# A graph layer's sort by destination group: whole quads sorted by 16 permute matmuls, or halves sorted by 8 and regrouped by DMA

## The chip, the cores and the metric

The kernel runs on one core of one Trainium2 chip. Times are microseconds (us) of the device for one execution; the median of the runs shown is compared. Engines: PE (TensorE), DVE (VectorE), ACT (ScalarE), POOL (GpSimd) and SP (SyncE, which issues most DMAs). SBUF is the on-chip memory with 128 partitions, PSUM holds the matmuls' sums.

## The reference

One message-passing layer on 6250 nodes of 128 features and 200,000 edges (`src`, `dst`, the latter sorted), with 20 edge features each:

```python
h = relu(layernorm(x))
x = h @ W_in
W_ij = (ssp(f_ij @ W_f1 + b_f1) @ W_f2 + b_f2) * f_ij_cutoff   # ssp(z) = softplus(z) - log 2
x_ij = x[idx_j] * W_ij                                         # a row of 128 for each edge
out = segment_sum(x_ij, idx_i, 6250)
result = x_in + (ssp(out @ W_o1 + b_o1) @ W_o2 + b_o2)
```

`idx_i` is `src` (in no order), `idx_j` is `dst` (sorted). So the gather reads neighbouring rows, and the sum over `src` scatters to anywhere.

## The kernel before, in words

**Quads.** The edges are taken in chunks of 128 and quads of 4 chunks (512 edges), 391 quads; two quads share one load of 1024 edges (`load_sc`, L338). One iteration of the main loop (L1325) handles one quad at each stage of a pipeline: in iteration i, quad i gets its one-hot matrix and filter exponentials, quad i-1 its messages, older quads the steps behind. The order of work on each engine is written out by hand: every step is put at an iteration and at a named point in it (`at`, `put`, the table `AT` at L34). The points run in the order L, D0, D1, PE0, PEZ, AE, A0, A1, AX, DM, DR, PE1, PE2, A2, D2, S (L1325 to L1379). Each engine, SP with its DMAs included, goes through its own part of this order without overtaking.

**Gather.** For each quad SP loads windows `wn` of 21 consecutive nodes (63 rows of a table in device memory, three bfloat16 parts to a node), one for each 256 edges (`WSEG`): 4 DMAs in a `load_sc`. The place comes from a register that SP loads from `base_i` and multiplies by 3 (L351 to L356). A one-hot matmul (`s2_pe_x`, L545) picks the rows, and DVE multiplies them with the filter (`s2_m`, L570): that is the messages.

**Scatter, three ways.** The first 12 "plain" quads that are not sorted merge edges of equal `src` within a chunk by an equality matrix (`s1_eq`, L401) and scatter-add 128 rows for each chunk. The other 188 plain quads are "listed": DVE compares the sources with `sb`, the row of sources broadcast to all partitions (`sb_load`, L386; `l_eq`, L419), edges with a repeated source go to a list, and the messages are scattered as they are. POOL issues each scatter as an indirect DMA with accumulation (`scatter`, L636), 4 for a quad, into one of up to four accumulators `acc` in device memory in turn (`acc_of`, L623: three in turn up to the 170th scatter, then four, and three again for the last 64).

**Sorting.** Every second quad from 8 to 388 (191 quads, `sorted_quads`, L1584) is sorted instead. The 6250 nodes make 16 groups of 392 (`GN`). `rank_group` to `rank_slot` (L645 to L713) give each of the 512 edges a slot: 32 (`CAP`) for each group, 512 in all, and 64 (`OVC`) more for what doesn't fit. `perm_oh` (L715) writes the one-hot matrix `pm`, 4 chunks x 576 columns. The messages are split in three bfloat16 parts (`part_rem`, L730) and carry their node number (`part_ext`). `permute` (L741) multiplies, for each of 4 blocks s of 128 slots, all 4 chunks: 16 matmuls of 387 columns. `perm_out` (L748) copies each block from PSUM by ACT to `ms` (one tile for each s). `over_pe` (L752) and the steps behind it take the overflow of two sorted quads as one more scatter of 128 rows. After 8 sorted quads (a round, `RND`), `unit_oh` and `unit_pe` (L820, L830) turn the sorted rows into sums: for each s 96 matmuls on 32 partitions each, a group to each 32, which DVE adds to `accT` in SBUF (`unit_evac`, L844). `unit_slots` (L1600) chooses the iterations of these units, the first of them `ULAG` = 5 after the round's last quad or the next free one.

**Sources.** `src16` in device memory holds the sources as int16, in the edges' order: `load_idx`, `src_cast` (L869, L890) make its first half at the start, `half_load`, `half_piece` (L1041, L1048) the second half in two pieces of the first iterations, together with the places `reld` of the destinations in their windows (`rel`, L938).

**End.** The accumulators are read back and summed, the output layers follow (L1478 on). If an edge found no slot or lay outside its window, a flag makes a slow loop over all 1563 chunks run (L1400 on).

Of the kernel before, what the change touches and what calls it, by code (L numbers as in the profile page):

```python
# [7 lines left out]
F32 = mybir.dt.float32  # L8
# [17 lines left out]
OVC = 64  # L26
SLOTS = GRP * CAP + OVC
# [5 lines left out]
ULAG = 5  # L33
AT = {  # L34
# [40 lines left out]
def tile_gnn(ctx: ExitStack, tc: tile.TileContext, x, fB, cT, srcT, srcr, srci, dstr, win_, wf1, wf2, bias, bo1c, wo1,  # L75
# [30 lines left out]
    mbufs = [max(len(qs) + sum(q > qs[-1] and (q + 3 if q + 4 in units else q + 4 + s // 2) <= us[s] for q in mpq) for qs, us in zip(rounds, uslots))  # L106
             for s in range(4)]
    splain = [q for q in range(NQ) if q not in mpi]
    plain = {q: n for n, q in enumerate(splain)}
    NS = len(splain)  # L110
    LB, LE = listed(NS) if spread else (0, 0)
# [68 lines left out]
    for i in range(2):  # L180
        ext_ = cp.tile([P, 4 * RKQ, 3], BF16, name=f"ext{i}")
        exts.append(ext_)
# [154 lines left out]

    def load_sc(s):  # L338
# [9 lines left out]
        for j in range(nh):  # L348
            nc.sync.dma_start(rb[j * HB:(j + 1) * HB], reld[s:s + 1, j * SEG:(j + 1) * SEG].to_broadcast([HB, SEG]))
        wn = ld.tile([P, 2, P], BF16, tag="wn", name="wn")  # L350
        _, regs = nc.values_load_multi_w_load_instructions(  # L351
            base_i[pp:pp + 1, hh, 0:2 * nh], engines=[SP], min_val=0, max_val=top,
            skip_runtime_bounds_check_because="clamped on the chip to [0, top]")
        for k in range(2 * nh):
            j, c = divmod(k, 2)
            nc.sync.dma_start(wn[j * HB:j * HB + NR, c, :], tab[bass.ds(regs[k] * 3, NR), :])  # L356
# [29 lines left out]
    def sb_load(k):  # L386
        qs = splain[2 * k:2 * k + 2]
        t_ = ld.tile([P, 2 * SEG], I16, tag="sb", name="sb", bufs=4)
        for j, q in enumerate(qs):
            if j and q == qs[0] + 1 and q % 2:  # L390
                continue
            n = 2 if j == 0 and len(qs) > 1 and qs[1] == q + 1 and q % 2 == 0 else 1
            o = q % 2 * SEG
            nc.sync.dma_start(t_[:, j * SEG:(j + n) * SEG],
                              src16[q // 2:q // 2 + 1, o:o + n * SEG].to_broadcast([P, n * SEG]))
        sbs[k] = t_
# [4 lines left out]
    def s1_eq(q):  # L401
# [3 lines left out]
        eq = wk.tile([P, 4, P], F32, tag="eq", name="eq", bufs=2)  # L405
# [139 lines left out]
    def s2_pe_x(q):  # L545
# [7 lines left out]
        for c in range(4):  # L553
            nc.tensor.matmul(xg[:, c, :], st[q]["oh"][a:a + NR, c * P:(c + 1) * P], wn[a:a + NR, c // 2, :],  # L554
# [114 lines left out]
    def before_me(ps_t, src, w, own=False):  # L669
        n = src.shape[1]  # L670
        nc.tensor.matmul(ps_t, trib if own else tri, src, start=True, stop=False)
        o = ps_t.rearrange("p (j c) -> p j c", c=4 * w)
# [1072 lines left out]
```

## Time and profile before

| | |
|---|---|
| median of 3 runs | 1914.89 us (1914.53 to 1915.02) |
| the profiled execution | 1913.11 us, its span 1911.3 us |
| instructions | 58065 |
| DMA packets | 351575, 267.55 MB |
| HBM | read 154.65 MB, written 109.00 MB |
| mean granted TensorE clock | 0.979 |

A profile is of one execution. "Busy" is the time in which an engine has an instruction under way. A group's row gives line, engine, operation, written tile <- read tiles, shape, count, then busy us, the mean of one in ns, and the idle time ahead of them with what ended it. Matmuls overlap, so the busy time over the count is what one costs, and the mean is how long one takes from end to end. In a list of waits each row says who waited, for what, us in total, how often, and the longest.

### The profile page before, as it was taken

To read this page: it belongs to the slowest core of one execution; us is meant where nothing else is said; L and a number is where in the kernel's file an instruction comes from. 1 tells how busy PE (TensorE), PEld (TensorE's weight loads), DVE (VectorE), ACT (ScalarE), POOL (GpSimd) and SP (SyncE) were. 2 spreads that over 40 slices of the span, in tenths; PEclk is the share of its full clock that TensorE was granted. 3 is DMA by queue.
4 is the path that set the end of the run, shared out by engine and by line. 5 is a ranking of instruction groups with operands and counts; after the bars stand their busy time and mean duration, and the time that the engine had idled before them with its cause. 6 is when DMAs were issued, how large, how long until landed. Compare 5 with 4: busy or idle time off the path is not lost. (4 is left out here: it accounts for less than half of the span.)

```text
span 1911.3 us, 58065 instructions
## 1 busy us (share of the span) xinstructions
PE 1809.2 (95%) x20601; PEld 1228.2 (64%) x20601; DVE 1655.9 (87%) x4692; ACT 1474.9 (77%) x4045; POOL 1509.0 (79%) x961
## 2 busy tenths in 40 slices
PE   4679999999999999999999999999999999999986
PEld 3556666666666666666666666666666666666654
DVE  5678998899999989999999889889889888888767
ACT  4569788878887878878887787787787787787725
POOL 4578777788888888887777888888888888878755
PEclk8789999999999999999999999999999999999998
DMA  8788777767776777776776667677676667666648
GB/s 287 201 208 167 142 162 135 131 125 131 139 135 123 131 126 130 129 152 116 125 135 126 124 126 129 118 129 129 116 130 129 116 130 127 117 117 133 106 99 269
DMA packets 351575, 267.55 MB, mean 140 GB/s; under 512 B 96655, under 2 KB 315194, under 8 KB 351282
## 3 DMA queue, kind: packets, MB, share of 16 engines
q1 hardware_dynamic: 218516, 197.56, 35.9%
q0 software_dynamic: 132208, 66.05, 34.6%
q8 instruction: 162, 2.65, 0.6%
q14 instruction: 131, 1.07, 0.2%
q10 hardware_dynamic: 558, 0.20, 0.0%
HBM read 154.65 MB, written 109.00 MB: 138 GB/s over the span
## 5 line engine op out<-in xcount | busy, mean ns | idle before, releaser
L639 POOL DMA_INDIRECT acc<-s,lji x751 | 1201.5, 1600 | 267.9 <-issue 174.4
L744 PE MATMUL pq<-pt,pm 128*128 128x387 bf16 x3056 | 583.2, 337 | 1.2 <-ACT s L597 0.6
L567 ACT ACTIVATE xc<-xg,cb 128x128 f32<-128x128 f32 x1564 | 448.1, 376 | 171.5 <-PE xg L554 151.9
L750 ACT CAST mst<-pq 128x387 bf16<-128x387 f32 x764 | 364.0, 487 | 91.7 <-PE pq L744 68.1
L562 PEld LDWEIGHTS W<-w,a 128*128 128x128 f32 x3128 | 421.7, 196 | 17.9 <-issue 7.3
L744 PEld LDWEIGHTS <-pm 128*128 128x128 bf16 x3056 | 294.4, 98 | 197.5 <-issue 4.9
L840 PE MATMUL un<-so,mst 32*128 32x392 bf16 x9168 | 411.3, 325 | 10.0 <-DVE rank L686 2.8
L562 PE MATMUL W<-w,a 128*128 128x128 f32 x3128 | 420.1, 278 | 0.0
L840 PEld LDWEIGHTS <-mst 32*128 32x128 bf16 x9168 | 249.8, 93 | 146.7 <-issue 19.0
L373 ACT ACTIVATE a<-a,con 128x512 f32<-128x512 f32 x391 | 282.5, 723 | 11.6
L733 DVE TENSOR_TENSOR pt<-pt 128x512 f32<-128x512 f32 x382 | 261.0, 683 | 0.0
L719 DVE TENSOR_SCALAR pm<-iotp,pos 128x576 bf16<-128x576 f16 x764 | 255.6, 396 | 0.0
L368 ACT ACTIVATE a<-z 128x512 f32<-128x512 f32 x391 | 236.6, 605 | 5.9 <-PE z L363 5.9
L851 DVE TENSOR_TENSOR accT<-un,accT 128x392 f32<-128x392 f32 x368 | 182.4, 558 | 63.1 <-PE un L840 34.8
L639 POOL DMA_INDIRECT acc<-os,oji x108 | 180.9, 1675 | 51.3 <-issue 12.9
L825 DVE TENSOR_SCALAR so<-iot,mst 128x392 bf16<-128x392 f16 x764 | 215.3, 333 | 2.2 <-PE un L840 1.9
L577 DVE TENSOR_TENSOR pt<-W,xc 128x512 f32<-128x512 f32 x191 | 131.6, 689 | 57.0 <-ACT xc L567 23.9
L363 PE MATMUL z<-ft,ws 123*128 123x512 bf16 x391 | 153.8, 394 | 19.9 <-POOL b2rep L979 8.4
L554 PE MATMUL xg<-wn,oh 63*128 63x128 bf16 x1564 | 156.6, 221 | 13.5 <-DVE oh L380 12.1
L577 DVE TENSOR_TENSOR s<-W,xc 128x512 f32<-128x512 f32 x188 | 128.7, 685 | 45.5 <-ACT xc L567 34.8
L551 PE MATMUL W<-b2rep,onesb 64*128 64x512 bf16 x391 | 152.9, 391 | 0.0
L639 POOL DMA_INDIRECT acc<-s,ji x48 | 81.0, 1688 | 42.1 <-DMA acc<-s,ji 20.5
(215 smaller groups left out, 1796.0 us busy)
## 6 DMA issues: line engine op xcount, KB each, us to landing
rb<-reld SPq DMA_DIRECT2D x391, 64.0 KB
sb<-src SPq DMA_DIRECT2D x192, 128.0 KB
fsd<-f SPq DMA_DIRECT2D x49, 480.0 KB
ft<-fsd SPq DMA_DIRECT2D x195, 120.0 KB
fb<-in_fB_dram SPq DMA_DIRECT2D x49, 320.0 KB
ft<-fsd SPq DMA_DIRECT2D x195, 80.0 KB
wn<-tab SPq DMA_DIRECT2D x782, 15.8 KB
acc<-s,lji POOLq DMA_INDIRECT x751
```

The lines of the kernel that those rows point to most:

```text
L368: nc.scalar.activation(a, st[q]["z"], AF.Exp)
L373: nc.scalar.activation(a, a, AF.Ln, bias=half, scale=0.5)
L562: nc.tensor.matmul(W[:, c, :], st[q]["a"][:, c * P:(c + 1) * P], w2, start=False, stop=(c == 3))
L567: nc.scalar.mul(xc[:, c, :], st[q]["xg"][:, c, :], late["c", q // CQ][:, 4 * (q % CQ) + c:4 * (q % CQ) + c + 1])
L577: nc.vector.tensor_tensor(m[:, :, :P], st[q]["W"], st[q]["xc"], op=ALU.mult)
L639: nc.gpsimd.indirect_dma_start(out=accs[k][:rows, :], out_offset=bass.IndirectOffsetOnAxis(ap=ji, axis=0), in_=s, in_offset=None, compute_ ...
L719: nc.vector.tensor_scalar(pm[:, c], iotp, rk[r]["pos"][:, 4 * j + c:4 * j + c + 1], None, op0=ALU.is_equal)
L733: nc.vector.tensor_tensor(pt[:, :, k * P:(k + 1) * P], a, high(a), op=ALU.subtract)
L744: nc.tensor.matmul(t[:, :PW], mp[q]["pm"][:, c, s * P:(s + 1) * P], high(mp[q]["pt"][:, c:c + 1, :PW])[:, 0], start=(c == 0), stop=(c == 3))
L750: nc.scalar.copy(mp[q]["ms", s][:, :PW], mp[q].pop(("q", s))[:, :PW])
L825: nc.vector.tensor_scalar(so, iotw[:, :GN], w[:, 3 * P // 2:3 * P // 2 + 1], None, op0=ALU.is_equal)
L840: nc.tensor.matmul(ts[g][:, :GN], mp[q]["ms", s][v, k * P:(k + 1) * P], mp[q]["oh"][v], start=(q == qs[0] and k == 0), stop=(q == qs[-1] a ...
```

## The change

Sorted quads are sorted in two halves of 256 edges. Each half has 16 slots (`BCAP`) for each of the 16 groups, 256 in all; overflow has 128 slots, shared by the four halves of two sorted quads. `pm` is 4 x 384. `permute` multiplies, for each half h and each of 2 blocks, the 2 chunks of that half: 8 matmuls of 388 columns. ACT copies the two blocks of a half into a staging tile `sg` (one of three buffers that `eq` has). Two DMAs of 64 partitions for each half (`regroup`), issued by SP, move whole rows of 1552 bytes from `sg` to every second partition of two tiles `ms`, so that 32 partitions again hold one group: 16 rows of the first half, 16 of the second. `regroup` stands at point A1 of iteration q+4 (first half) and q+5 (second); where q+4 is a unit's iteration, all permutes stand in q+3 as before and both regroups at point L of q+4. `ULAG` is 7. `ms` has 11 and 15 buffers of 1552 bytes a partition, where the four tiles had 9, 11, 13 and 15 of 776.

The source rows are put into the plain quads' order on the host: 100 rows, cast once at the start by POOL; `sb_load` is one DMA of both quads. The second half's source loads and casts go.

In the first half of the edges (196 quads) a window serves 512 edges: 2 `wn` DMAs in a `load_sc` in place of 4. `base_3` holds the places times 3, so SP multiplies nothing.

The diff, cut to its core:

```diff
-OVC = 64
-SLOTS = GRP * CAP + OVC
+BCAP = 16
+OVC = 128
+SLOTS = GRP * BCAP + OVC
-ULAG = 5
+ULAG = 7
+    "rg0": (4, "A1"), "rg1": (5, "A1"),
-             for s in range(4)]
+    mbufs = [max(len(qs) + sum(q > qs[-1] and q + 5 <= us[2 * j + 1] for q in mpq) for qs, us in zip(rounds, uslots))
+             for j in range(2)]
+    def seg_of(s):
+        return SEG if spread and s < HALF else WSEG
...
-            base_i[pp:pp + 1, hh, 0:2 * nh], engines=[SP], min_val=0, max_val=top,
-        for k in range(2 * nh):
-            j, c = divmod(k, 2)
-            nc.sync.dma_start(wn[j * HB:j * HB + NR, c, :], tab[bass.ds(regs[k] * 3, NR), :])
+            base_3[pp:pp + 1, hh, 0:m * nh], engines=[SP], min_val=0, max_val=3 * top,
+        for k in range(m * nh):
+            j, c = divmod(k, m)
+            nc.sync.dma_start(wn[j * HB:j * HB + NR, c, :], tab[bass.ds(regs[k], NR), :])
...
     def sb_load(k):
-            nc.sync.dma_start(t_[:, j * SEG:(j + n) * SEG],
-                              src16[q // 2:q // 2 + 1, o:o + n * SEG].to_broadcast([P, n * SEG]))
+        nc.sync.dma_start(t_[:, :n], src16[k:k + 1, :n].to_broadcast([P, n]))
...
-    def before_me(ps_t, src, w, own=False):
+    def before_me(ps_t, src, w, m, own=False):
...
-        nc.vector.tensor_scalar(ov, rank, float(BIG + CAP), None, op0=ALU.is_ge)
+        nc.vector.tensor_scalar(ov, rank, float(BIG + BCAP), None, op0=ALU.is_ge)
...
-    def permute(q, s):
-        for c in range(4):
-            nc.tensor.matmul(t[:, :PW], mp[q]["pm"][:, c, s * P:(s + 1) * P], high(mp[q]["pt"][:, c:c + 1, :PW])[:, 0],
-                             start=(c == 0), stop=(c == 3))
+    def permute(q, k):
+        h, s = divmod(k, 2)
+        for c in (2 * h, 2 * h + 1):
+            nc.tensor.matmul(t[:, :MW], mp[q]["pm"][:, c, s * P:(s + 1) * P], high(mp[q]["pt"][:, c:c + 1, :MW])[:, 0],
+                             start=(c == 2 * h), stop=(c == 2 * h + 1))
-    def perm_out(q, s):
-        mp[q]["ms", s] = wk.tile([P, MW], BF16, tag=f"ms{s}", name="mst", bufs=mbufs[s])
-        nc.scalar.copy(mp[q]["ms", s][:, :PW], mp[q].pop(("q", s))[:, :PW])
+    def perm_out(q, k):
+        h, s = divmod(k, 2)
+        if s == 0:
+            mp[q]["sg", h] = wk.tile([P, 2, MW], BF16, tag="eq", name="sg", bufs=3)
+        nc.scalar.copy(mp[q]["sg", h][:, s], mp[q].pop(("q", k))[:, :MW])
+    def regroup(q, h):
+        sg = mp[q].pop(("sg", h))
+        for j in range(2):
+            if h == 0:
+                mp[q]["ms", j] = wk.tile([P, 2, MW], BF16, tag=f"ms{j}", name="mst", bufs=mbufs[j])
+            nc.sync.dma_start(mp[q]["ms", j][h::2].rearrange("p s f -> p (s f)"),
+                              sg[j * HB:(j + 1) * HB].rearrange("p s f -> p (s f)"))
     def over_pe(q):
-        for c in range(4):
-            for h, p in enumerate(qs):
-                nc.tensor.matmul(t[h * OVC:(h + 1) * OVC, :PW], mp[p]["pm"][:, c, GRP * CAP:],
-                                 high(mp[p]["pt"][:, c:c + 1, :PW])[:, 0], start=(c == 0), stop=(c == 3))
+        for p in qs:
+            for c in range(4):
+                nc.tensor.matmul(t[:, :PW], mp[p]["pm"][:, c, GRP * BCAP:], high(mp[p]["pt"][:, c:c + 1, :PW])[:, 0],
+                                 start=(p == qs[0] and c == 0), stop=(p == q and c == 3))
...
-                    nc.tensor.matmul(ts[g][:, :GN], mp[q]["ms", s][v, k * P:(k + 1) * P], mp[q]["oh"][v],
+                    nc.tensor.matmul(ts[g][:, :GN], mp[q]["ms", s // 2][v, s % 2, k * P:(k + 1) * P], mp[q]["oh"][v],
...
+                for h in range(2):
+                    at(q + 4, "L", regroup, q, h)
...
+                for h in range(2):
+                    put(f"rg{h}", q, regroup, q, h)
...
-        "srci": srcp.reshape(-1, 2, P).transpose(0, 2, 1).reshape(-1, SC),
+        "srci": srcp.reshape(-1, 2, P).transpose(0, 2, 1).reshape(-1, SEG)[order].reshape(-1, SC),
```

More of the change, by code (lines that the diff above doesn't have):

```diff
@@ L110, in tile_gnn @@
     NS = len(splain)
+    SR = -(-NS // 2)
     LB, LE = listed(NS) if spread else (0, 0)
@@ L667, in rank_local @@
         rk[r]["ext"] = ext
[L669 removed]
+    def before_me(ps_t, src, w, m, own=False):
         n = src.shape[1]
         nc.tensor.matmul(ps_t, trib if own else tri, src, start=True, stop=False)
[L672 to L675 removed]
+        parts = []
+        a = n // (m * w) * m * w
+        if a:
+            parts.append((0, a, m))
+        if a < n:
+            parts.append((a, n, (n - a) // w))
+        for a, b, c in parts:
+            o = ps_t[:, a:b].rearrange("p (j c) -> p j c", c=c * w)
+            v = src[:, a:b].rearrange("p (j c) -> p j c", c=c * w)
+            for k in range(1, c):
+                nc.tensor.matmul(o[:, :, k * w:], onesb, v[:, :, :(c - k) * w], start=False,
+                                 stop=(b == n and k == c - 1))
     def rank_count(r):
```

95 lines of the change are left out of this document (43 added, 52 removed), and 2 rows, old and new, of the table AT.

## The prediction

> **What bounds the kernel now.** I read the page's busy line first, then busy time by stage, then what POOL waits for in each stage, and the groups by line last.
>
> ```profile
> PE 1809.2 (95%) x20601; PEld 1228.2 (64%) x20601; DVE 1655.9 (87%) x4692; ACT 1474.9 (77%) x4045; POOL 1509.0 (79%) x961
> ```
>
> By this line TensorE is the bound: it is busy for 95% of the span of 1911.3 us, POOL for 79%. By stage it looks otherwise. The columns are stretch and length, then busy us (and instructions) of PE, PEld, DVE, ACT, POOL, the granted clock, the DMA share and GB/s.
>
> ```profile
> 90.00:400.00 310.00, 294.30 (x3221) 199.34 (x3220) 271.07 (x786) 251.25 (x702) 245.92 (x152) 0.98 0.78 157
> 400.00:800.00 400.00, 391.87 (x4562) 265.90 (x4564) 367.25 (x1082) 325.13 (x907) 335.96 (x211) 1.00 0.72 131
> 1200.00:1700.00 500.00, 495.70 (x5840) 332.92 (x5829) 440.47 (x1232) 403.96 (x1106) 416.73 (x256) 1.00 0.69 124
> ```
>
> POOL's waits between 400 and 800 us (waited for: us in total, times, longest):
>
> ```profile
> POOL acc L639 <- issue: 44.8, 147, 0.3
> POOL acc L639 <- DMA acc<-s,lji: 7.6, 25, 0.3
> ```
>
> No wait there is longer than 0.3 us, and 0.3 us stands ahead of every scatter: it belongs to the instruction. So 211 scatters of 335.96 / 211 = 1.59 us and 0.30 us each are 399 of the 400 us. POOL is saturated there. Between 800 and 1700 us it isn't quite:
>
> ```profile
> POOL acc L639 <- DVE s L577: 25.3, 25, 2.3
> POOL acc L639 <- DVE srcf L650: 3.5, 2, 2.4
> POOL acc L639 <- DVE bn L234: 2.3, 2, 2.0
> ```
>
> Less 0.3 us for each of the 29 times, 31.1 - 8.7 = 22.4 us is real waiting for a message that DVE had yet to make. From 1700 to 1840 us:
>
> ```profile
> POOL acc L639 <- DVE s L577: 6.6, 5, 4.1
> POOL acc L639 <- DMA acc<-s,lji: 6.5, 7, 3.0
> POOL acc L639 <- ACT pt L739: 4.3, 2, 3.6
> ```
>
> This is 10.9 - 2.1 = 8.8 us for messages, and 4.4 us for earlier scatters. Two engines are thus level: PE at 98 to 99% of every stage and POOL within 3% of it. Time taken from PE alone can bring back only what POOL waits for PE's results, some 31 us, and not what PE is relieved of.
>
> **The change part by part.** The groups (busy us, mean ns; the z row is of 300 to 1800 us alone):
>
> ```profile
> L639 POOL DMA_INDIRECT acc<-s,lji x751 | 1201.5, 1600 | 267.9 <-issue 174.4 <-DVE s L577 33.4 <-DMA acc<-s,lji 28.0
> L639 POOL DMA_INDIRECT acc<-os,oji x108 | 180.9, 1675 | 51.3 <-issue 12.9 <-DMA acc<-s,lji 9.7 <-ACT oji L814 9.4
> L639 POOL DMA_INDIRECT acc<-s,ji x48 | 81.0, 1688 | 42.1 <-DMA acc<-s,ji 20.5 <-issue 7.6 <-ACT a L368 5.5
> L744 PE MATMUL pq<-pt,pm 128*128 128x387 bf16 x3056 | 583.2, 337 | 1.2 <-ACT s L597 0.6 <-ACT mst L750 0.6
> L757 PE MATMUL po<-pt,pm 128*64 128x387 bf16 x764 | 86.6, 344 | 7.7 <-DVE accT L851 4.0 <-DVE so L825 1.7 <-issue 1.0
> L719 DVE TENSOR_SCALAR pm<-iotp,pos 128x576 bf16<-128x576 f16 x764 | 255.6, 396 | 0.0
> L733 DVE TENSOR_TENSOR pt<-pt 128x512 f32<-128x512 f32 x382 | 261.0, 683 | 0.0
> L825 DVE TENSOR_SCALAR so<-iot,mst 128x392 bf16<-128x392 f16 x764 | 215.3, 333 | 2.2 <-PE un L840 1.9 <-issue 0.3
> L750 ACT CAST mst<-pq 128x387 bf16<-128x387 f32 x764 | 364.0, 487 | 91.7 <-PE pq L744 68.1 <-issue 19.1
> L363 PE MATMUL z<-ft,ws 123*128 123x512 bf16 x329 | 128.1, 389 | 4.0 <-DVE pt L577 4.0
> ```
>
> The z row gives the pace: 1500 us / 329 = 4.56 us for a quad, 9.12 us for a pair (one sorted, one listed).
>
> *TensorE.* A permute multiplies 2 chunks in place of 4: 1528 of 3056 matmuls go, at 583.2 / 3056 = 0.191 us, so -292 us. The overflow matmuls stay 764 but are 128 columns wide; at 64 wide two of them share the array and one costs 86.6 / 764 = 0.113 us. Between 0.113 and 0.191 I take 0.191, the row of that width: +60 us. PE falls to about 1577 us.
>
> *VectorE.* pm has 384 columns for 576. By columns 255.6 us becomes 170, so -85 us; if the fixed part were all of it, 0. I take -75. DVE then has some 1580 us.
>
> *ScalarE.* The 764 copies at L750 keep their size. Nothing.
>
> *POOL.* All 751 + 108 + 48 = 907 scatters remain. They and their 0.3 us are 1463 + 272 = 1735 us, which PE at 1577, DVE at 1580 and ACT at 1475 no longer reach: POOL alone becomes the bound from its first scatters on. The waits for messages go: -22 us (800 to 1700) and -9 us (1700 to 1840). What is late next is POOL's own last scatter, and the chain behind it (list rows read back, summed, scattered, tail), which I leave as it is. Nothing is gained from 400 to 800 us, where nothing waited.
>
> *Sources and windows.* Sorting the source rows on the host makes one DMA of each pair of sb, and one window for each of the first 196 quads takes 196 wn DMAs away. The casts of the second half leave DVE, one tiny multiplication comes. All of this is on SP and DVE, which have room: 0 us, and at most the 1 us that SP's shorter first loads may bring at the start.
>
> *The regroup.* 191 x 4 = 764 DMAs of 64 rows x 1552 bytes, 75.9 MB, are new. They have two costs, on SP and on the DMA engines. Rows of the DMA view, and two pairs of SP's timeline (start, us, what):
>
> ```profile
> q1 hardware_dynamic: 218516, 197.56, 35.9%
> sb<-src SPq DMA_DIRECT2D x192, 128.0 KB
> wn<-tab SPq DMA_DIRECT2D x782, 15.8 KB
> ```
> ```profile
> 1005.46 0.91 SPq L394 DMA_DIRECT2D sb<-src  x2
> 1047.69 1.88 SPq L349 DMA_DIRECT2D rb<-reld  x2
> 1052.51 1.09 SPq L345 DMA_DIRECT2D ft<-fsd  x3
> 1053.69 1.11 SPq L349 DMA_DIRECT2D rb<-reld  x2
> 1055.87 1.76 SPq L356 DMA_DIRECT2D wn<-tab  x4
> ```
>
> No transfer from SBUF to SBUF is in the trace, so both prices are bounded. On SP an issue lies between 0.36 (ft) and 0.56 us (rb, also 64 rows); I take 0.5, nearer to rb. A pair now holds SP for 1.09 + 1.11 + 1.76 us, up to 1.1 us between rb and wn, and some 0.5 us of sb: 5.5 us. With four regroups 7.5 us, under 9.12. In SP's order the first two wait for ACT's copies at A0 of iteration q+4 and the others at q+5, and behind them stand the loads of the next iterations, which are needed three iterations later (13 us): that is their cover. Twice in each 16 iterations a regroup has to wait for the unit matmuls to release its ms buffer; SP then stands until the end of that iteration, when the same cover has some 8 us left. If the cover were gone, PE would stop, but POOL would still have the messages of up to six s buffers to scatter.
>
> On the DMA engines the new share is 48,896 / 218,516 x 35.9% = 8% by packets or 75.9 / 197.56 x 35.9% = 14% by bytes. I take 11%, between the two since 1552 bytes is above q1's mean of 904; the wn that go give back under 1%. The share goes from 0.72 to about 0.82. That matters to POOL, which waits for an earlier scatter into the same accumulator. Between 90 and 400 us, with three accumulators in turn and a share of 0.78:
>
> ```profile
> POOL acc L639 <- DMA acc<-s,lji: 13.8, 17, 2.2
> POOL acc L639 <- DMA acc<-s,ji: 6.3, 7, 2.5
> POOL acc L639 <- DMA acc<-os,oji: 1.7, 2, 0.8
> ```
>
> Less 26 x 0.3 us this is 14.0 us on 152 scatters. With 11% more traffic I take it at 23, +9 us (bounds 0 and +30). From 400 us on four accumulators take turns, and no wait is over 0.3 us even at 0.72: 0 there.
>
> *POOL's own speed.* Three scatters, and DVE at that time:
>
> ```profile
> 1121.08 2.01 POOL L639 DMA_INDIRECT acc<-os,oji  x1 [0.30 <-ACT mst L750]
> 1123.39 1.54 POOL L639 DMA_INDIRECT acc<-s,lji  x1 [0.30 <-DVE ovs L771]
> 1125.24 1.69 POOL L639 DMA_INDIRECT acc<-s,lji  x1 [0.30 <-issue]
> ```
> ```profile
> 1118.15 1.20 DVE L719 TENSOR_SCALAR pm<-iotp,pos 128x576 bf16<-128x576 f16 x4
> 1120.99 0.69 DVE L733 TENSOR_TENSOR pt<-pt 128x512 f32<-128x512 f32 x1
> 1125.14 1.40 DVE L719 TENSOR_SCALAR pm<-iotp,pos 128x576 bf16<-128x576 f16 x4
> ```
>
> A scatter takes 1.54 us undisturbed; 2.01 with an L733 begun just before it, 1.69 beside four pm instructions, which then take 1.40 in place of 1.20. All scatters together lose 1463.4 - 907 x 1.54 = 67 us so. If L733, L719 and L825 share that by their 732 busy us, pm has 23 us of it, and a third of it goes with its columns: 8 us. The sharing is a guess, so I take half: -4 us.
>
> The Trainium skill, in "SBUF — State Buffer", section "Who interferes with whom", says that DVE instructions in a two-port mode, tensor_scalar among them, take a port pair that POOL needs too, and that whichever comes second waits for the whole of the other. The trace agrees in kind (2.01 and 1.69 against 1.54 us). Taken fully, with all of pm's share gone, the sum below would be 19 us lower.
>
> The sum on the profiled execution's own time: 1913.1 - 22 - 9 + 9 - 4 = 1887 us. The median of the runs shown, 1914.89, is 1.8 us above that execution, so 1889.
>
> **The rivals.** *The scatters land late (slower).* Place: POOL's wait for an accumulator, after 400 us. If 0.82 of DMA share brought there what 0.78 brings in the three-accumulator stage, 14.0 / 152 = 0.09 us a scatter, the other 737 scatters would cost 66 us, and the time would be 1955; with half of it 1922. It decides from 26 us on. For it: POOL has no slack left once it is the bound, so each wait counts. Against it: four accumulators leave 4 x 1.9 = 7.6 us for a landing, not 5.7, and 0.72 shows nothing over 0.3.
>
> *SP becomes the bound (slower).* If a regroup took SP over (9.12 - 5.5) / 4 = 0.9 us, loads would set the pace. The row of 1.88 us for two rb shows that 0.94 occurs; if it were usual, 5.5 + 3.8 = 9.3 us a pair, 191 x 0.18 = 34 us longer than now, 1949. The ordinary 1.11 speaks against it.
>
> *Something else keeps the pace (no change).* Messages pass PE, ACT, DVE and PE again in an order written by hand; a pair could stay at 9.1 us though no engine is full, for DVE has 367 of 400 us busy and ACT's copies wait 68 us for the permutes. Then 1915. Against it: DVE loses 0.4 us a pair, and hardly any PE wait is recorded.
>
> *POOL itself gets faster.* All of pm's 23 us: 1889 - 19 = 1870.
>
> *The change does not do what it says.* If more than 128 edges of two sorted quads found no slot, or a window passed 21 nodes, the loop over 1563 chunks would run. Counted from the inputs that the reference draws, the fullest two quads have exactly 128, and the widest of the first 196 quads spans 18 nodes. With one scatter of 1.54 us to a chunk at the least, it would add over 2400 us.
>
> **How the numbers follow.** My forecast gets 0.59, the faster POOL 0.10, no change 0.12, late landing 0.14, SP 0.04, the loop 0.01. A difference under 0.2% (4 us) is no difference here. So faster 0.69, same 0.12, slower 0.19. The likeliest case alone reaches from 1871 (no further DMA waits, twice the port gain, 5 us off the end chain) to 1910 (+30 of DMA waits). The range goes to 1860, which takes in the faster POOL at 1870 with some 10 us of the end chain and the DMA waits beside it, and to 1922 for no change and for late landing by half; what lies above is left out.
>
> **What would show it.** Right: L744 with 1528 matmuls and about 290 us, pm near 170 to 180 us; PE's busy share down to 83 or 85%; POOL with the highest share of all between 400 and 1800 us, waits for DVE s near zero, its rows "issue" alone; q1 some 73 MB larger, DMA share above 0.8. Wrong: POOL still waiting for s (the pace is kept elsewhere); POOL's waits for acc over 0.3 us after 400 us (late landing); SP without waits for PE and PE waiting for ft, rb or wn (SP); scatters far from 1.6 us; any fallback loop. A time under 1860 or over 1922 would break the sum.

## The result, and the profile after

| | before | after |
|---|---|---|
| median | 1914.95 us (1914.53 to 1917.84, 4 runs) | 1927.81 us (1927.09 to 1931.52, 4 runs) |
| the profiled execution | 1913.11 us, span 1911.3 us | 1931.52 us, span 1929.8 us |
| mean granted TensorE clock | 0.979 | 0.964 |

The ratio is 1.0068 (95% interval 1.005 to 1.0085): slower by 0.7%, and above the range of the prediction. The page's busy line and its line of the DMA queue q1, after:

```profile
PE 1681.8 (87%) x19124; PEld 1149.9 (60%) x19124; DVE 1596.0 (83%) x4692; ACT 1456.0 (75%) x4045; POOL 1512.8 (78%) x961
q1 hardware_dynamic: 251248, 269.74, 49.3%
```

TensorE has 127 us less to do and VectorE 60, and yet the span is 18.5 us longer. Three of the stages that the prediction shows, in the same columns:

```profile
90.00:400.00 310.00, 267.39 (x2831) 183.14 (x2832) 257.63 (x780) 241.47 (x683) 248.43 (x154) 0.95 0.88 188
400.00:800.00 400.00, 367.29 (x4392) 250.94 (x4394) 360.85 (x1094) 329.74 (x930) 336.78 (x208) 0.99 0.86 173
1200.00:1700.00 500.00, 447.94 (x5258) 302.70 (x5255) 410.02 (x1202) 390.23 (x1081) 402.77 (x248) 0.99 0.81 163
```

From 400 to 800 us POOL is as full as before (336.78 us busy for 335.96). From 1200 to 1700 us no engine in the row is full any more: PE is busy for 448 of 500 us, DVE for 410, and POOL for only 403 where it had 417. What POOL waits for from 800 to 1700 us (in total, times, longest):

```profile
POOL acc L639 <- issue: 101.6, 333, 0.3
POOL acc L639 <- ACT pt L747: 30.0, 18, 4.3
POOL acc L639 <- DMA acc<-s,lji: 10.1, 33, 0.3
POOL acc L639 <- DVE s L577: 4.4, 8, 1.0
```

The waits for DVE's messages, 25.3 us before, are nearly gone. In their place stand 30.0 - 18 x 0.3 = 24.6 us behind ACT. DVE and ACT wait in turn; over the whole run:

```profile
DVE s L577 <- ACT xc L567: 147.3, 80, 4.5
ACT sg L761 <- DMA mst<-sg: 124.6, 63, 6.3
```

The first row was 34.8 us before. The second is new: ACT's copy of a sorted block waits for a staging tile `sg`, and what releases that tile is the regroup that read it (`mst<-sg`). One such place on the timeline (start, us, engine and line, operation, count, idle time ahead), SP first, then ACT, DVE and POOL:

```profile
1119.14 2.43 SPq L768 DMA_DIRECT2D mst<-sg  x4
1121.62 1.35 SPq L350 DMA_DIRECT2D ft<-fsd  x3
1123.07 1.14 SPq L354 DMA_DIRECT2D rb<-reld  x2
1125.27 2.49 SPq L362 DMA_DIRECT2D wn<-tab  x4
1127.86 2.41 SPq L768 DMA_DIRECT2D mst<-sg  x4
1130.37 1.32 SPq L350 DMA_DIRECT2D ft<-fsd  x3
```
```profile
1126.33 0.87 ACT L761 CAST sg<-pq 128x388 bf16<-128x388 f32 x2
1131.11 0.87 ACT L761 CAST sg<-pq 128x388 bf16<-128x388 f32 x2 [3.90 <-DMA mst<-sg]
1131.86 0.62 ACT L374 ACTIVATE a<-z 128x512 f32<-128x512 f32 x1
1133.14 1.13 ACT L567 ACTIVATE xc<-xg,cb 128x128 f32<-128x128 f32 x4
```
```profile
1134.30 0.69 DVE L577 TENSOR_TENSOR s<-W,xc 128x512 f32<-128x512 f32 x1 [3.67 <-ACT xc L567]
```
```profile
1134.90 1.54 POOL L639 DMA_INDIRECT acc<-os,oji  x1 [0.95 <-ACT pt L747]
```

SP works without a stop. The tile that ACT needs is freed by the first two of the four regroups that start at 1127.86 us. ACT had filled that tile by 1121.20 us, but ft, rb and wn, the loads of a later pair, stood ahead of them on SP. ACT stands for 3.90 us until they have landed, with the filter's exponential and the messages' copies `xc` queued behind; DVE gets its `xc` 3.67 us late, and POOL's next overflow scatter comes late as well. SP's own waits between 300 and 1800 us, before:

```profile
SPq L356 <- PE z L363: 259.6, 87, 6.3
SPq L335 <- DVE f L334: 48.2, 27, 3.2
```

and after:

```profile
SPq L768 <- ACT sg L761: 24.5, 47, 2.1
SPq L350 <- PE pq L753: 12.5, 25, 1.2
```

Before, SP stood for 260 us because the buffers that it loads were still in use: it ran ahead of the others. After, hardly anything holds it. I summed every SP instruction of the trace in these 1500 us, with the register loads (one TENSOR_LOAD for each `load_sc`, on average 0.75 us before and 0.83 after) and the gaps under 0.15 us in which the sequencer goes from one instruction to the next; "idle" is what is left:

| 300 to 1800 us | instructions | short gaps | idle | SP's time for a pair of quads |
|---|---|---|---|---|
| before | 969 us | 150 us | 381 us (25%) | 6.83 us |
| after | 1275 us | 183 us | 42 us (3%) | 8.94 us |

A pair takes 1500 / 163 = 9.20 us after. So SP's queue is full to 97%. (The instructions include semaphore rows of over 0.15 us, in which SP stands waiting: 32 us of them before, 5 us after.)

The average hides two different halves of the edges. I took the time between the register loads of loads 20 and 90, which after the change bring one window for a quad, and of loads 100 and 185, which bring two. "Pace" is the time for a pair, "SP" its instructions and short gaps:

| us for a pair | first half: pace | SP | second half: pace | SP |
|---|---|---|---|---|
| before | 9.27 | 7.14 | 8.96 | 6.58 |
| after | 9.00 | 8.67 | 9.19 | 9.06 |

In the first half SP keeps 0.33 us for a pair in hand, and shortly behind the middle the changed kernel is still ahead: its 500th scatter ends at 1037.0 us, before at 1044.2. In the second half SP alone needs 9.06 us for a pair, more than the whole pair took before, and the lead is lost: the 850th scatter ends at 1743.0 us, before at 1733.0, and the last at 1873.1 for 1859.1.

### The profile page after: what moved, and what is told of

The parts are those of the page before. It is cut to its first block, busy times and chain, and to the rows that moved or that the text cites. A ratio compares the mean times of both kernels' runs of the same rounds, so it can differ in the third digit from the quotient of the medians.

```text
span 1929.8 us, 55808 instructions
## 1 busy us (share of the span) xinstructions
PE 1681.8 (87%) x19124; PEld 1149.9 (60%) x19124; DVE 1596.0 (83%) x4692; ACT 1456.0 (75%) x4045; POOL 1512.8 (78%) x961
## 3 DMA queue, kind: packets, MB, share of 16 engines
q1 hardware_dynamic: 251248, 269.74, 49.3%
## 5 line engine op out<-in xcount | busy, mean ns | idle before, releaser
L639 POOL DMA_INDIRECT acc<-s,lji x751 | 1217.7, 1621 | 241.2 <-issue 174.7
L855 PE MATMUL un<-so,mst 32*128 32x392 bf16 x9168 | 446.3, 332 | 50.2 <-ACT sg L761 42.4
L761 ACT CAST sg<-pq 128x388 bf16<-128x388 f32 x764 | 344.4, 491 | 160.3 <-DMA mst<-sg 124.6
L562 PE MATMUL W<-w,a 128*128 128x128 f32 x3128 | 429.0, 282 | 0.0
L855 PEld LDWEIGHTS <-mst 32*128 32x128 bf16 x9168 | 263.8, 95 | 207.2 <-issue 74.7
L753 PE MATMUL pq<-pt,pm 128*128 128x388 bf16 x1528 | 321.6, 335 | 20.5 <-ACT os L820 6.2
L577 DVE TENSOR_TENSOR s<-W,xc 128x512 f32<-128x512 f32 x188 | 129.2, 687 | 159.8 <-ACT xc L567 147.3
L639 POOL DMA_INDIRECT acc<-os,oji x108 | 171.9, 1591 | 83.1 <-ACT pt L747 43.6
L753 PEld LDWEIGHTS <-pm 128*128 128x128 bf16 x1528 | 143.4, 97 | 124.5 <-issue 32.2
L727 DVE TENSOR_SCALAR pm<-iotp,pos 128x384 bf16<-128x384 f16 x764 | 201.7, 325 | 0.0
L577 DVE TENSOR_TENSOR pt<-W,xc 128x512 f32<-128x512 f32 x191 | 130.4, 683 | 46.1 <-ACT xc L567 17.2
L776 PE MATMUL po<-pt,pm 128*128 128x387 bf16 x764 | 150.4, 338 | 0.6 <-DVE ldup L439 0.5
```

The lines of the kernel that those rows point to most:

```text
L562: nc.tensor.matmul(W[:, c, :], st[q]["a"][:, c * P:(c + 1) * P], w2, start=False, stop=(c == 3))
L577: nc.vector.tensor_tensor(m[:, :, :P], st[q]["W"], st[q]["xc"], op=ALU.mult)
L639: nc.gpsimd.indirect_dma_start(out=accs[k][:rows, :], out_offset=bass.IndirectOffsetOnAxis(ap=ji, axis=0), in_=s, in_offset=None, compute_ ...
L727: nc.vector.tensor_scalar(pm[:, c], iotp, rk[r]["pos"][:, 4 * j + c:4 * j + c + 1], None, op0=ALU.is_equal)
L753: nc.tensor.matmul(t[:, :MW], mp[q]["pm"][:, c, s * P:(s + 1) * P], high(mp[q]["pt"][:, c:c + 1, :MW])[:, 0], start=(c == 2 * h), stop=(c ...
L761: nc.scalar.copy(mp[q]["sg", h][:, s], mp[q].pop(("q", k))[:, :MW])
```

## The experiments

Theory A: SP's issue queue is full, so regroups are issued late, the staging tiles come back late, and ACT stands. Rivals: B, the 76 MB of new traffic slow every transfer and POOL; C, three staging tiles are too few, whatever SP does. "Before" is the kernel before, run on the same chip as the experiment: 1914.7 to 1916.5 us (medians). The changed kernel was measured beside 1914.95 us, so a difference to its 1927.81 us can carry some 2 us of the chips. SP's idle time and its time for a pair are those of the first table above. A profile is of one execution, which can lie some 10 us off the median.

**One DMA for a regroup** (the same bytes, half the issues; the rows of the two halves of a quad are not interleaved, so groups do not come together).

```diff
-        for j in range(2):
-            ...
-            nc.sync.dma_start(mp[q]["ms", j][h::2].rearrange("p s f -> p (s f)"),
-                              sg[j * HB:(j + 1) * HB].rearrange("p s f -> p (s f)"))
+        mp[q]["ms", h] = wk.tile([P, 2, MW], BF16, tag=f"ms{h}", name="mst", bufs=mbufs[h])
+        nc.sync.dma_start(mp[q]["ms", h].rearrange("p s f -> p (s f)"), sg.rearrange("p s f -> p (s f)"))
```

> Each half of a sorted quad is moved from staging to its ms tile by one DMA of 128 rows in place of two of 64; all bytes and packets stay. The rows are not interleaved, so the units add rows of the wrong groups (the output is not the reference's); every other instruction stays. Theory A (SP's queue is full, the issues themselves are the bound): two issues of about 0.6 us less for each pair of quads, SP gets about 1.2 us of 9.15 us back, POOL becomes the bound, time 1885 to 1895 us, ACT's wait for staging under 30 us of the 125 us. Theory B (the load on the DMA engines, share 0.85 and up, is the bound): bytes are the same, time 1920 to 1930 us. Theory C (three staging buffers are too few for the landing time): a single issue lands a little earlier, time 1910 to 1920 us.

Measured: 1900.45 us (1899.29 to 1908.88), ratio 0.9934 (0.9914 to 0.9955) to before, 27 us under the changed kernel: 5 us above theory A's range and 10 us or more below the others'. ACT's wait for staging falls from 124.6 to 49.6 us, not to under 30. SP idles for 211 us and waits for others again, and POOL from 800 to 1700 us has no wait over 0.8 us:

```profile
SPq L337 <- DVE f L336: 61.4, 31, 4.4
SPq L362 <- PE z L369: 32.2, 21, 3.9
```
```profile
POOL acc L639 <- issue: 106.4, 349, 0.4
POOL acc L639 <- DMA acc<-s,lji: 11.3, 37, 0.3
```

So with half the issues POOL is the bound that the prediction had in mind, at all of the new bytes. (The packets of q1 are not quite the same, 245,136 for 251,248, and the DMA share from 400 to 800 us is 0.83 for 0.86.)

**Half the bytes** (the same 764 issues; only one of the two blocks of a half is moved, and both unit steps read that one).

```diff
-            nc.sync.dma_start(mp[q]["ms", j][h::2].rearrange("p s f -> p (s f)"),
-                              sg[j * HB:(j + 1) * HB].rearrange("p s f -> p (s f)"))
+            nc.sync.dma_start(mp[q]["ms", j][h::2, 0], sg[j * HB:(j + 1) * HB, 0])
...
```

> All four regroup DMAs of a quad stay, but each moves only the first of the two blocks (776 bytes a row, half the bytes, the same number of packets); the units read that block twice, so half of the sorted sums are left out (the output is not the reference's). Theory A (SP's issues): the issues stay, time 1915 to 1930 us, SP still without gaps. Theory B (load on the DMA engines): the share falls by some 5 points, a good part of the new load goes, time about 1900 us or less. Theory C: landing gets some 0.2 us shorter, 1920 to 1928 us.

Measured: 1907.83 us (1900.21 to 1913.10), ratio 0.9965 (0.9949 to 0.998); 20 us under the changed kernel, between A's range and B's. In the profile, which is of the fastest execution, an issue costs SP about the same, 0.597 us on average for 0.606, and SP still idles for 37 us only, but a pair holds it for 8.80 us in place of 8.94. So the bytes have an effect too, 20 us where half the issues gave 27, with intervals that overlap. By size all of it could go by way of SP, whose other loads are issued a little faster: 0.14 us for each of 191 pairs is 27 us. How much is landing time instead, this run does not tell.

**Four staging tiles** in place of three (and as many of the other tiles that share these buffers).

```diff
-            mp[q]["sg", h] = wk.tile([P, 2, MW], BF16, tag="eq", name="sg", bufs=3)
+            mp[q]["sg", h] = wk.tile([P, 2, MW], BF16, tag="eq", name="sg", bufs=4)
```

> The changed kernel with four staging buffers in place of three, nothing else. Theory C (the buffers): ACT gets half an iteration pair, some 4.6 us, more before it must wait, which is more than the mean wait of 2.0 us; the wait of 125 us falls under 40 us, the time to 1890 to 1900 us. Theory A (SP's issues): SP has no gap to catch up in, so the backlog only grows to the next limit; 1922 to 1930 us. Theory B (DMA load): about 1925 us as well.

Measured: 1923.55 us (1917.53 to 1934.66), ratio 1.0064 (1.0041 to 1.0087). ACT's wait for staging falls from 124.6 to 18.6 us, and other waits grow, the first of these two from 48.6 us, the second from 10.6:

```profile
ACT os L532 <- PE lsum L527: 95.7, 12, 12.1
PE lsum L526 <- DMA lm<-acc: 54.5, 17, 8.6
```

The wait has moved to the list rows `lm`, which SP loads too; SP idles for 32 us. The time is A's (1922 to 1930 us), and C falls: the staging tile was where the full queue showed, not its cause.

**Two windows again** in the first half of the edges: 196 more small DMAs on SP, the rest of the change kept.

```diff
     def seg_of(s):
-        return SEG if spread and s < HALF else WSEG
+        return WSEG
```

> The changed kernel with a window for each 256 edges in the first half too (the window part of the change undone): 196 more small DMAs, two for each pair of quads in the first half, 0.35 to 0.4 us each with their register steps. Theory A (SP's issues): SP, with 4% of its time free there, is 0.75 us a pair over; 98 pairs, so 40 to 70 us longer, 1965 to 2000 us. Theory B (DMA load): 3 MB more, under 1% of the share, at most 5 us, 1925 to 1935 us. Theory C (staging buffers): about the same as the change, 1925 to 1935 us.

Measured: 1984.40 us (1980.44 to 1988.44), ratio 1.0351 (1.0328 to 1.0375). That is 57 us more than the changed kernel, or 0.29 us for each added wn, close to what one such issue costs SP on average here (0.31 us). The loss lies where the loads were added: in the first half a pair takes 9.56 us and holds SP for 9.35 (9.00 and 8.67 without them), in the second 9.20 and 9.06 as in the changed kernel. A load that cost next to nothing before is paid for almost in full now.

```profile
ACT sg L761 <- DMA mst<-sg: 169.3, 78, 10.0
```

**Without the halves**: the kernel before with only the source rows in the plain quads' order and one window in the first half.

```diff
+    def seg_of(s):
+        return SEG if spread and s < HALF else WSEG
...
+        nc.sync.dma_start(t_[:, :n], src16[k:k + 1, :n].to_broadcast([P, n]))
```

> The kernel before with the other two parts of the change alone: the source rows in the plain quads' order and one window for 512 edges in the first half; whole quads are sorted as before, no regroup. Theory A (SP's queue is full only with the regroups): SP had some 17% of its time in waits for PE before, so taking 0.4 to 1.0 us a pair from it brings nothing; 1911 to 1917 us. Theory B (DMA load counts by itself): the load hardly changes, the same time as well. A time under 1908 us would say that SP or these loads bound the kernel before too.

Measured: 1908.99 us (1907.91 to 1912.41), ratio 0.9961 (0.9948 to 0.9974). These two parts are worth 0.4%, 7.5 us, a little more than was expected (2 us under that range, but above the 1908 us that would have spoken for SP). A pair holds SP for 6.28 us, in both halves alike (6.29), and SP idles for 470 us; PE is the full engine again:

```profile
1200.00:1700.00 500.00, 494.37 (x5842) 331.43 (x5844) 440.88 (x1231) 405.17 (x1105) 415.49 (x255) 1.00 0.68 123
```

**Overflow scatters left out**, with one DMA for a regroup: 96 scatters less for POOL.

```diff
-    for q in mpq[1::2] + mpq[-1:] * (len(mpq) % 2):
-        scat[q + 10] += 1
...
-                k = put("over_int", k, over_int, q)
-                at(k, "S", over_scatter, q)
+                put("over_int", k, over_int, q)
```

> The kernel with one regroup DMA for each half, with the 96 scatters of overflow rows left out (their sums are missing from the output, and the rows are still not interleaved). What bounds the kernel once SP has room? If POOL does, as the prediction had it: 96 x 1.92 = 184 us less of POOL, down to what DVE (1598 us busy) and SP (about 7.9 us a pair) allow, 1760 to 1830 us. If a chain of waits between PE, ACT and DVE keeps the pace: 1885 to 1900 us, hardly less than the 1900 us with these scatters. If SP still does: 1890 to 1900 us as well, with SP without gaps.

Measured: 1852.13 us (1837.28 to 1854.74), ratio 0.9641 (0.9609 to 0.9673): between the ranges for POOL and for the chain. POOL is busy for 1368.3 us in place of 1514.8; with 0.30 us for each scatter it has 175 us less to do, and the time falls by 48 us. Then POOL waits for messages:

```profile
POOL acc L637 <- DVE s L575: 147.0, 86, 9.1
```

So the chain of the other engines lies only some 50 us under POOL. SP idles for 220 us there and is not what holds it.

**One load of places** for both quads of a pair (391 rb issues become 196; both quads' windows lie in the same 64 partitions, DVE makes the one-hot matrix for each quad, `sb` has three buffers in place of four).

```diff
-        rb = ld.tile([P, SEG], BF16, tag="rb", name="rb")
-        for j in range(nh):
-            nc.sync.dma_start(rb[j * HB:(j + 1) * HB], reld[s:s + 1, j * SEG:(j + 1) * SEG].to_broadcast([HB, SEG]))
+        rb = ld.tile([HB, SC], BF16, tag="rb", name="rb")
+        nc.sync.dma_start(rb[:, :n], reld[s:s + 1, :n].to_broadcast([HB, n]))
...
```

> The changed kernel with SP relieved at another place: the two rows of places that a load brings go side by side into 64 partitions by one DMA in place of two, both quads' windows stand in the same partitions, and DVE makes the one-hot matrix of each quad by itself (one more instruction of about 0.3 us a pair); the sb buffers go from 4 to 3 for space. Theory A (SP's issues): 0.6 us a pair less, 8.5 us in place of 9.15, under POOL's 8.75; POOL becomes the bound, 1898 to 1908 us, faster than both kernels. Theory B (DMA load): bytes and packets nearly the same, 1920 to 1930 us.

Measured: 1935.57 us (1926.92 to 1937.68), ratio 1.0088 (1.007 to 1.0106): above the ranges of both theories. SP is relieved (149 us idle), and POOL's waits from 400 to 1700 us are down to 1 us beyond the 0.3 us of each scatter, as A has it; but POOL itself is slower:

```profile
L635 POOL DMA_INDIRECT acc<-s,lji x751 | 1251.3, 1666 | 243.6 <-issue 186.0 <-DMA acc<-s,lji 23.7 <-DVE accT L862 6.3
```

A scatter takes 1666 ns in place of 1622 (with one DMA for a regroup), and POOL is busy for 1556.0 us in place of 1514.8: 41 us, where that kernel was 35 us faster. My guess was that the 195 additional DVE instructions disturb POOL; a later run, with the one-hot matrix in two DVE instructions, tries it.

**A quarter of the regroups from ACT.**

```diff
-            nc.sync.dma_start(mp[q]["ms", j][h::2].rearrange("p s f -> p (s f)"),
+            (nc.scalar if h and q + 4 not in units else nc.sync).dma_start(mp[q]["ms", j][h::2].rearrange("p s f -> p (s f)"),
```

> The changed kernel with a quarter of the regroup DMAs (the second half's two, for the quads whose regroups stand at two points) issued by ACT in place of SP; the same transfers. Theory A (SP's issues): SP gets 0.6 us a pair back, ACT loses as much and had 25% to spare; 1900 to 1912 us. Theory B (DMA load): the same load, 1922 to 1932 us. If ACT's place in the chain of messages is what counts, the 0.6 us on ACT cost more than they bring: over 1925 us.

Measured: 1957.34 us (1948.38 to 1962.96, and one run of 2253.7 that nothing in a profile explains), ratio 1.0202 (1.0179 to 1.0226). SP idles for 167 us, but each of these issues now stands in ACT's own order, for 0.596 us on average, and ACT makes the copies `xc` that the messages wait for. DVE's wait for `xc` in the sorted quads rises from 17.2 to 86.3 us:

```profile
DVE pt L577 <- ACT xc L567: 86.3, 46, 5.0
```

In the listed quads it falls, from 147.3 to 44.6 us. So the loss of 30 us is measured; that ACT's place in the chain is its cause is argued from the order of work, and this list of waits does not show it.

**ft in two DMAs** in place of three, with the changed kernel otherwise whole: a test of A that touches no regroup, and a version that could win.

```diff
-FPARTS = ((0, 3), (3, 2), (5, 1))
+FPARTS = ((0, 4), (4, 2))
-    fsd = dp.tile([NB, 3, RB * BE], BF16, name="fsd")
+    fsd = dp.tile([NB, 4, RB * BE], BF16, name="fsd")
-        nc.sync.dma_start(fsd[b].rearrange("g (p e) -> p g e", p=P), f3)
+        for k in (1, 2):
+            nc.sync.dma_start(fsd[b, 2 * k - 2:2 * k].rearrange("g (p e) -> p g e", p=P), f3[:, 0:k + 1:k])
-    part = np.array([0, 0, 0, 1, 1, 2])
+    part = np.array([0, 0, 1, 0, 2, 1])
```

> The changed kernel with the filter inputs ft of a load_sc in two DMAs (80 and 40 rows) in place of three (60, 40, 20); for that the first of the three parts is written twice to fsd, by one more DMA for each of its 49 blocks (7.8 MB more in all). Regroups untouched. SP loses 195 issues and gets 49: at 0.43 us (three ft in 1.30 us) some 63 us, 0.33 us of the 9.1 us of a pair. If SP's issue queue is what sets the pace: faster than the changed kernel by most of what halving the regroup issues gave, 1903 to 1915 us. If the DMA load is it: no gain or a small loss, 1925 to 1935. If the staging tiles or the order of the chain are it: 1923 to 1932.

Measured: 1896.85 us (1892.39 to 1910.70), ratio 0.991 (0.9884 to 0.9936) to before: 31 us under the changed kernel and 6 us under the range that was expected of the queue, with 8 MB more to move (q1 277.76 MB). In the profile, which is of an execution of 1906.26 us, a pair holds SP for 8.76 us; 0.18 us less for each of 191 pairs is 34 us. POOL from 800 to 1700 us, and the stage from 1200 us on:

```profile
POOL acc L640 <- issue: 110.1, 361, 0.3
POOL acc L640 <- DMA acc<-s,lji: 11.0, 36, 0.3
POOL acc L640 <- DVE f L336: 2.1, 5, 0.9
```
```profile
1200.00:1700.00 500.00, 454.10 (x5412) 307.85 (x5411) 422.45 (x1232) 398.91 (x1107) 418.99 (x262) 0.99 0.86 172
```

POOL has 419 us again (403 in the changed kernel) and waits for hardly anything: it is the bound. SP is close behind, with 54 us idle. 147 of the 2781 DMAs that SP issues decide it, at a DMA share of 0.86 for the changed kernel's 0.81 and with the most bytes on q1 of all these kernels. B as the main cause falls with that.

**The same, and 73 loads from ACT** (the raw filter inputs and the cutoffs).

```diff
-        nc.sync.dma_start(t_, fB[b].rearrange("r e -> (r e)").rearrange("(p e) -> p e", p=P))
+        nc.scalar.dma_start(t_, fB[b].rearrange("r e -> (r e)").rearrange("(p e) -> p e", p=P))
...
-        nc.sync.dma_start(t_[:, :n], cT[:, 4 * CQ * b:4 * CQ * b + n])
+        nc.scalar.dma_start(t_[:, :n], cT[:, 4 * CQ * b:4 * CQ * b + n])
```

> As the kernel with ft in two DMAs, and besides the loads of the raw filter inputs (49) and of the cutoffs (24) are issued by ACT in place of SP: SP loses some 40 us more, 0.55 us a pair in all. Issue queue: 1898 to 1910 us, at POOL's level or near it, unless ACT's in-order chain pays for the 73 issues (each at most 1 us of ACT, which is busy for 75%). DMA load: 1925 to 1935.

Measured: 1919.65 us (1913.65 to 1932.72), ratio 1.0023 (1.0006 to 1.0041): above the queue's range, 23 us over the kernel without this edit. SP idles for 83 us in place of 54. DVE's waits for `xc`, here in the listed and in the sorted quads, were 121.8 and 22.7 us without the edit:

```profile
DVE s L578 <- ACT xc L568: 104.7, 87, 4.5
DVE pt L578 <- ACT xc L568: 53.6, 35, 4.8
```

Together they grow by 14 us. That ACT pays for the 73 issues in its order fits, as with the regroups, but is not shown to be all of the loss.

**The one-hot matrix in two DVE instructions**, with one DMA for a regroup: the DVE part of the kernel with one load of places, by itself.

```diff
-            nc.vector.tensor_scalar(oh[v], rb[v], rowid[v], None, op0=ALU.is_equal)
+            for j in range(min(2, NQ - q)):
+                v = slice(j * HB, (j + 1) * HB)
+                nc.vector.tensor_scalar(oh[v], rb[v], rowid[v], None, op0=ALU.is_equal)
```

> The kernel with half the regroup issues, and the one-hot matrix of each load_sc made by two DVE instructions of 64 partitions in place of one of 128: 195 DVE instructions of 512 elements more, nothing else (the rows of the two halves of a quad are not interleaved, as in the kernel with half the issues). It tells why the kernel with one load of places for both quads was slow. If more DVE instructions of this kind lengthen POOL's scatters: scatters of 1.66 to 1.72 us in place of 1.62 and 1925 to 1945 us. If that kernel lost its time by the single load of 64 rows or the third buffer less for sb: 1899 to 1908.

Measured: 1905.53 us (1900.66 to 1910.56, and one run of 5271.9 that no profile shows), ratio 0.9942 (0.9925 to 0.996), 5 us over the kernel without the edit, which is within the two intervals. DVE has 93 us more to do, and scatters take 1629 ns in place of 1622:

```profile
L641 POOL DMA_INDIRECT acc<-s,lji x751 | 1223.3, 1629 | 248.6 <-issue 173.2 <-DMA acc<-s,lji 32.6 <-DVE oh L388 8.4
L388 DVE TENSOR_SCALAR oh<-rb,con 64x512 bf16<-64x512 bf16 x391 | 149.7, 383 | 7.6 <-DMA rb<-reld 1.6
```

My guess falls: the DVE instructions are 7 of the 44 ns at most. Whether the rest comes of windows that all lie in 64 partitions, or of the missing `sb` buffer, was not tried and stays open.

**ft in two DMAs in the kernel before**, as a control.

> The kernel before with ft in two DMAs and the first part written twice, as in the kernel with ft in two DMAs, and nothing else of the change. In the kernel before SP waits some 360 us between 300 and 1800 us, so its 150 issues less are worth nothing if what they are worth is room in SP's issue queue: 1911 to 1919 us. If two larger ft transfers are better in themselves (they land earlier, or fewer of them disturb others): 1890 to 1902 here too.

Measured: 1912.33 us (1908.71 to 1914.57), ratio 0.9988 (0.9979 to 0.9997). The edit that is worth 31 us where SP is full is worth 2 where SP idles for over a quarter of the time (423 us here). So it is the room in SP's queue that counted.

## Why the prediction was wrong

**The step that failed** is the SP term of the regroup: "A pair now holds SP for 1.09 + 1.11 + 1.76 us, up to 1.1 us between rb and wn, and some 0.5 us of sb: 5.5 us. With four regroups 7.5 us, under 9.12." It was built from the rows of two pairs. Over 1500 us the kernel before holds SP for 6.83 us a pair: the two pairs showed no load of the raw filter inputs, of the cutoffs, the lists or the table, and the short gaps between instructions are 0.92 us a pair. Sources and windows give 0.55 us back (6.28 us without the halves), where I had taken 0. Four regroups add 8.94 - 6.28 = 2.66 us, 4 x 0.606 of them the issues themselves, where I had 2.0. So 8.94 us, 97% of a pair, and not 82%. (The 6.28 us hold 0.26 us of the waiting that stands in semaphore rows, the 8.94 us hardly any, so the regroups add rather more than 2.66.) In the second half of the edges, where most of the stretch from 800 to 1700 us lies, it is worse: 6.29 us without the halves and 2.77 us of regroups are 9.06, where the forecast, 22 us less on the 99 pairs of that stretch, asks for a pace of some 8.96 - 0.23 = 8.73 us.

**The cover was looked for on the wrong side.** I named what is queued behind a regroup on SP (loads with 13 us in hand) and not what stands ahead of it. By the trace a regroup is issued 5.1 us (median; 0.8 to 9.0 for 90% of them) after ACT's copy is done, and until it has landed it holds one of three staging tiles, for which ACT waits. PE's waits for ft, rb or wn, which I had named as the sign, did not have to come first: ahead of the z matmuls the wait for ft is 14.6 us after, for 4.2 before.

**The rival "SP becomes the bound"** had the right engine with too little weight, 0.04. Its point of decision, 0.9 us a regroup, hung on the 5.5 us. With the SP time of the kernel without the halves it is (9.12 - 6.28) / 4 = 0.71 us over the whole stretch, where 2.66 / 4 = 0.67 was measured, just under it; in the second half it is (8.96 - 6.29) / 4 = 0.67, and 2.77 / 4 = 0.69 was measured, just over it. Both terms of my sum were too small: the base (6.28 for 5.5), and the regroup, whose issue alone costs 0.606 us and lies above the 0.36 to 0.56 by which I bounded it. The rival's price was 34 us over the kernel before; the changed kernel is 13 us over it, and 27 to 31 us over the two kernels that relieve SP.

The Trainium skill, in "Perfetto Trace Analysis", section "What 'DMA-bound' means", names the sequencer of the issuing engine as a bound of its own, seen as a track of solid DMA slices that stand for the making of descriptors and not for the moving of data. The trace agrees: SP's track is 97% taken (register loads and short gaps among it), and an issue costs 0.597 us at half the bytes and 0.606 us at all of them. The same page of the Trainium skill, in its section "DMA Optimizations", says that spreading DMAs over several issuing engines may help in that case. It did not here: the two runs that gave some to ACT were 23 us slower than without it (two ft) and 30 us slower (a quarter of the regroups).

**POOL as the next bound** was right once SP has room: 1900.45 and 1896.85 us against the 1889 forecast. By terms, in the kernel with two ft: the -22 us (800 to 1700) came, for POOL's real waits there are down from 22.4 to 1.9 us. The -9 us (1700 to 1840) did not come; its overflow scatters wait for ACT there. What follows POOL's last scatter, which I had left as it is, grew from 52.3 us before to 58.1 (60.4 with one DMA for a regroup). The +9 us of DMA waits before 400 us did not come either: in the changed kernel 10.8 + 7.7 + 3.4 us in 25 waits, 14.4 us beyond their 0.3 us, for 14.0 before, though the DMA share rose from 0.78 to 0.88. I had taken 11 points for the new traffic; q1's share rose by 13, from 35.9 to 49.3%, nearer to the 14 that I had worked out by bytes, and from 400 to 800 us the share is 0.86, not 0.82. Late landing did not happen for all that: from 400 to 1700 us no wait for `acc<-s,lji` is over 0.3 us in the changed kernel.

**Sizes.** Groups after:

```profile
L639 POOL DMA_INDIRECT acc<-s,lji x751 | 1217.7, 1621 | 241.2 <-issue 174.7 <-DMA acc<-s,lji 24.7 <-DVE s L577 7.5
L753 PE MATMUL pq<-pt,pm 128*128 128x388 bf16 x1528 | 321.6, 335 | 20.5 <-ACT os L820 6.2 <-DVE oeq L807 2.0 <-ACT r L247 2.0
L776 PE MATMUL po<-pt,pm 128*128 128x387 bf16 x764 | 150.4, 338 | 0.6 <-DVE ldup L439 0.5
L727 DVE TENSOR_SCALAR pm<-iotp,pos 128x384 bf16<-128x384 f16 x764 | 201.7, 325 | 0.0
```

A permute matmul costs 0.210 us for 0.191, in chains of two in place of four (-262 us, not -292); the overflow +64 us, as taken; pm -54 us, not -75: 0.264 us for 384 columns and 0.335 for 576. TensorE falls by 127 us, not by 232, for other groups grow: the 9168 unit matmuls, which I left at their cost, take 446.3 us where they took 411.3. They go with the same shortage: PE waits 42.4 us ahead of them behind ACT's copies to staging; with one DMA for a regroup that wait is 1.0 us and they take 409.2, with two windows it is 63.9 and they take 466.2. (The first stage that I showed, from 90 to 400 us, has PE at 95%, so it was not at 98 to 99% of every stage.) The sources and windows, which I had at 0 to 1 us, are worth 7.5 us by themselves. And the -4 us for POOL's own speed did not come: its scatters of messages take 1621 ns after and 1600 before, with a third of pm's columns gone, and all 907 scatters together 6 us more. So the 19 us that the prediction worked out for the case that POOL loses all of pm's share are not borne out here; whether the heavier DMA traffic hides a part of them, no run separates.

## What to carry to other kernels

Before DMAs are added to an engine that issues them, add up that engine's instructions over a long stretch, register loads and the gaps between instructions included, and compare with the pace; two neighbouring rows of its timeline are not enough, and its waits for free buffers are the reserve. Do this for each stretch with a different load: here the average left 3% of room, and the half that decided left 1%. Ask of a DMA that frees a buffer what stands ahead of it in its queue, not only what stands behind. When a queue is full, remove or join issues anywhere in it: here two ft in place of three, in a part that the change never touched, turned 0.7% slower into 0.9% faster than before.

## What was not expected of the hardware

The issue of a regroup on SP has a price for each DMA and hardly one for its size: 0.606 us on average for 64 rows of 1552 bytes, 0.597 us for 64 rows of 776, 0.602 us for 128 rows of 1552. Other loads cost 0.32 us (wn, 63 rows) to 0.57 us (rb, 64 rows) in the changed kernel. A register load for the places of a pair costs SP 0.83 us, more than any of these. A regroup adds 16 packets beyond its rows: against the kernel without the halves, q1 has 61,120 packets more, 80 for each of the 764 DMAs of 64 rows, and 55,008 with one DMA for a regroup, 144 for each of 382. In the kernel with all windows in 64 partitions scatters took 1666 ns in place of 1622, with the cause open. And the granted TensorE clock was lower where PE had less to do: 0.95 from 90 to 400 us after the change (PE busy for 267 us), 0.98 before (294 us).
